# A cap on the token scatters under way in the second attention stage

## The chip, the cores and the metric

The kernel runs on one core of one Trainium2 chip. The metric is the time of one execution on the device in microseconds (us), as the median of several runs. A profiled execution is a separate run, from which the trace and the profile come.

## The reference, cut to what matters

The program is a deformable convolution with a residual, then an attention block, then a mixture of experts, on an input of 4 images of 256 channels and 64 x 64 positions. After the attention each of the 4 x 4096 = 16,384 tokens (256 values) is normalised, and a router picks two of eight experts for it:

```python
def _moe(tokens, router_w, w1, b1, w2, b2):
    logits = tokens.astype(jnp.float32) @ router_w.astype(jnp.float32).T
    probs = jax.nn.softmax(logits, axis=-1)
    rw, re = jax.lax.top_k(probs, TOP_K)                 # TOP_K = 2
    rw = rw / jnp.maximum(rw.sum(-1, keepdims=True), 1e-12)
    combine = jnp.zeros((N, E), tokens.dtype).at[jnp.arange(N)[:, None], re].set(rw)
    out = tokens
    for e in range(E):                                   # E = 8
        h = jax.nn.gelu(tokens @ w1[e] + b1[e], approximate=False)
        out = out + combine[:, e:e + 1] * (h @ w2[e] + b2[e])
    return out
```

Everything is float32. The kernel does not multiply all tokens by all experts: it sorts each token's row to the two experts that it chose.

## The kernel before, in words

The work runs in four stages, one after the other with small overlaps.

1. The deformable convolution. POOL (GpSimd) gathers four corners of each sample by indirect DMAs (L626), VectorE weighs them (L651), PE transposes and multiplies (L665, L690).
2. The first attention stage (from L819): statistics, queries and keys, and the 4 x 4 attention weights `att` between the images for each head.
3. The second attention stage (L1071 to L1509), which the change touches. `block(j)` (L1291) is called for j = 0 to 7; a block is 512 positions of all four images, 2,048 tokens or 16 tiles of 128. For each block PE makes the values and the gates (`value`, `gate`, both through `project`, L796), ScalarE and VectorE mix the images (`spread` L1091, `mixed` L1098), VectorE gates (`gated`, L1118), PE multiplies by the output matrix (`output`, L1129), VectorE adds the residual (`added`, L1146), and ScalarE takes squares (`squares`, L1165). The routing of block j - 1 is woven into block j: POOL raises the variances to the power -1/2 (`rstd`, L1178, twice a block), VectorE makes the shift (L1185) and picks two experts (`pick`, L1206 to L1224), ScalarE normalises the rows into the tile `u` (`normed`, L1193), PE counts tokens by expert (`count`, L1238), and VectorE turns that into row numbers (`placed`, L1252 to L1264).
4. The experts (from L1516): 142 tiles of 256 sorted rows are fetched (`fetch`, L1531), multiplied (`hidden` L1577, `result` L1595), and their results are scattered back (L1606).

A scatter (`scatter`, L1273) is an indirect DMA that POOL issues: it writes the 128 rows of one tile, 260 words each, to the rows `xs_rows` in DRAM whose numbers stand in `slots`. There are 16 tiles and 2 choices for each of 8 blocks, so 256 scatters; `placed` puts 32 of them in the list `waiting`, and `scatter(n)`, called at fixed places in `block`, takes up to n of them from it. The scatters of the last block are issued one for each expert tile in stage 4 (L1737).

What sets the order: in the second attention stage the order of VectorE, ScalarE, PE and SyncE is that of the text (`manual_schedule`, L836); POOL's is left to the scheduler. `in_turn` (L181) adds edges of order, without a wait, between the scatters and the `rstd` instructions: `scatter` puts each scatter behind the last `rstd` issued, and `rstd` goes behind all the scatters issued since the one before. In stage 4 POOL's order is that of the text too.

All scatters write to one of two DRAM tensors. They write disjoint rows, so each is declared to be free of dependencies towards the others in a group named "scatter" (L1281, L1282).

The DMAs that POOL issues take turns on eight semaphores, and each waits, before it is issued, for the earlier one that counted on its own semaphore.

Of the kernel before, what the change touches and what calls it, by code (L numbers as in the profile page):

```python
# [67 lines left out]
RELOADED = -(-(NE * WROW + SPARE * HALF) // (B * STATE))  # L68
FETCH = 3
XTS, YS = 5, 4  # L70
NG = B * NT


# [5 lines left out]
def conv_attn_moe_kernel(  # L79
# [101 lines left out]
    def in_turn(ins, others):  # L181

        for other in others if not fixed else ():
            tc.add_manual_dep(
                ins.ins, other.ins.name,
                mybir.DependencyInfo(mybir.DependencyClass.NoSync, mybir.DependencyReason.DATA),
                reason="order of issue",
            )
# [36 lines left out]
    with ExitStack() as actx:  # L225
# [482 lines left out]
        with tc.manual_schedule(engines=order):  # L708
# [7 lines left out]
            for n in range(total + 2):  # L716
# [22 lines left out]
                if n % 2 == 0 and n + NGB < total:  # L739
# [6 lines left out]
                        reason="the next gather's buffer",  # L746
# [266 lines left out]

    gates = route_pool.tile([P, NBLK, 2, NG], F32, name="gates")
    rank_i = route_pool.tile([P, NE], I32, name="rank_i")
# [16 lines left out]

    same_expert = route_pool.tile([P, NE, NG], F32, name="same_expert")
    G.memset(same_expert, 1.0)
# [14 lines left out]
    def over_experts(ap):  # L1049
        return ap.unsqueeze(2).to_broadcast([P, NG, NE])  # L1050

    def over_tiles(ap):
        return ap.unsqueeze(1).to_broadcast([P, NG, NE])

    def first_max(pool, lg, name, which):

        m = pool.tile([P, NG], F32, name=f"m{which}_{name}", tag=f"top_m{which}")
        V.tensor_reduce(m, lg, AX.X, ALU.max)
        oh = pool.tile([P, NG, NE], F32, name=f"oh{which}_{name}", tag=f"top_oh{which}", bufs=1)
        V.tensor_tensor(oh, lg, over_experts(m), ALU.is_equal)  # L1060
# [10 lines left out]
    with ExitStack() as bctx:  # L1071
# [172 lines left out]

        waiting = []
        scattered = []

        def placed(j):
            pp, oh1, oh2 = picked.pop(j)
            base = bases[j - 1] if j % HB else base0  # L1250
            pos = bs.tile([P, NG, NE], F32, name=f"pos{j}", tag="lg", bufs=1)
            V.tensor_tensor(  # L1252
                pos, pp[:, : NE * NG].rearrange("p (e n) -> p n e", n=NG), over_tiles(base),
                ALU.add,
            )
            after = bs.tile([P, NE], F32, name=f"base{j}", tag="base")
            V.tensor_tensor(after, pp[:, NE * NG : NE * NG + NE], base, ALU.add)
            bases[j] = after
            slots = bs.tile([P, 2, NG], I32, name=f"slots{j}", tag="slots")
            for k, oh in enumerate((oh1, oh2)):  # L1260
                V.tensor_tensor(oh, oh, pos, ALU.mult)
                row = bs.tile([P, NG], F32, name=f"row{j}_{k}", tag="row")
                V.tensor_reduce(row, oh, AX.X, ALU.add)
                V.tensor_copy(slots[:, k], row)  # L1264
            waiting.extend(
                (us[j, n // NT], slots, n, k, xs_rows[j // HB])
                for n in range(NG) for k in range(2)
            )

        def scatter(most):  # L1270
            for _ in range(min(most, len(waiting))):
                u, slots, n, k, rows_ = waiting.pop(0)
                s = G.indirect_dma_start(  # L1273
                    out=rows_,
                    out_offset=bass.IndirectOffsetOnAxis(ap=slots[:, k, n : n + 1], axis=0),
                    in_=u[:, n % NT, :], in_offset=None,
                )
                in_turn(s, issued[-1:])
                scattered.append(s)

                tc.declare_no_dep(s.ins, group="scatter", reason="disjoint rows")  # L1281
                tc.add_to_no_dep_group("scatter", s.ins)  # L1282
# [8 lines left out]
        def block(j):  # L1291
# [25 lines left out]
            mixed(j, 1, 1, [2, 3])  # L1317
            spread(j, 0, [1, 0])
            scatter(3)
            scatter(10)  # L1320
            mixed(j, 1, 1, [0])
            gate(j, 1, 1)
# [18 lines left out]
            value(j, 2, 0)  # L1341
            mixed(j, 3, 0, [0])
            scatter(13)
            mixed(j, 3, 0, [2])
            mixed(j, 2, 0, [1])
# [447 lines left out]
```

## Time and profile before

| what | us |
|---|---|
| three timed runs | 3581.35, 3588.42, 3590.16 |
| their median | 3588.42 |
| the profiled execution | 3621.63 |
| its span, from the first instruction to the last | 3619.9 |
| convolution, until the last gather (L626) | to about 2114 |
| first attention stage | about 2114 to 2392 |
| second attention stage, until its last `rstd` pair begins | about 2392 to 2917 |
| experts and output | from about 2917 on |

How to read the profile: PE is the matrix engine and PEld its weight load, DVE is VectorE, ACT is ScalarE, POOL is GpSimd, SP is SyncE; a "q" behind an engine's name (POOLq) is its sequencer, which waits and issues. A group line gives source line, engine, operation, what it writes and reads, the count, then its busy time and the mean of one in ns, and then the time that the engine stood idle just before such instructions and who ended that idle time. "issue" there means that the profile shows nothing that was waited for; "remote" or "an unknown queue" means that a semaphore was waited for whose update the profile cannot assign to an instruction. The row of an indirect DMA on POOL is the time of its issue by POOL; the packets of the data stand in the view of the DMA engines.

### The profile page before, as it was taken

The numbers are of one execution on the slowest core, as the hardware profiler recorded it, in microseconds if no ns is written. First come the engines' busy times: TensorE is split into PE (matmuls) and PEld (weight loads), VectorE is DVE, ScalarE is ACT, GpSimd is POOL, SyncE is SP. The second block draws the span as 40 slices with busy tenths as digits, with TensorE's granted clock in tenths as the row PEclk, the third lists the DMA queues.
The fourth block names the chain that finished last, engine by engine and source line by source line (L and its number), as shares of the span: only waits on it lengthen the run. The fifth ranks groups of instructions, "written<-read, shape, count | busy, mean of one in ns | idle before, by whom it ended". The sixth has DMA issues, their size and how long they took to land.

```text
span 3619.9 us, 49496 instructions
## 1 busy us (share of the span) xinstructions
PE 3041.8 (84%) x13658; PEld 2230.4 (62%) x13658; DVE 2480.5 (69%) x6303; ACT 1832.4 (51%) x4281; POOL 1961.6 (54%) x1818
## 2 busy tenths in 40 slices
PE   5899997899987899977777889997676588899996
PEld 4667665667665676656566655543343367788884
DVE  5867686777776777866666758875445555455887
ACT  2556554456554565544444457744344254455663
POOL 2555565666576665677666643305445536655441
PEclk8999998999998999989888989998788789999996
DMA  9889889899989899988787878723234334444888
GB/s 301 306 304 336 316 326 351 278 353 366 348 313 350 307 346 341 352 297 310 280 312 285 320 205 141 139 74 121 99 105 154 111 97 132 154 138 153 289 280 285
DMA packets 349897, 911.66 MB, mean 252 GB/s; under 512 B 43540, under 2 KB 123035, under 8 KB 347576
## 3 DMA queue, kind: packets, MB, share of 16 engines
q0 software_dynamic: 208704, 689.10, 55.1%
q1 hardware_dynamic: 140920, 219.39, 19.0%
q8 instruction: 113, 1.85, 0.2%
q14 instruction: 160, 1.31, 0.1%
HBM read 741.87 MB, written 170.12 MB: 252 GB/s over the span
## 4 chain that ended last, share of the span: by engine, by line
PE 48%; issue 14%; POOL 11%; DMA 9%; DVE 8%; another core or an unknown queue 6%; ACT 3%; SPq 0%; POOLq 0%; DVEq 0%; ACTq 0%
PE acc L690 13%; POOL g L626 10%; DMA g<-table,idx 6%; PE ph L1577 6%; PE py L1595 5%; PE tps L665 3%; PE po L433 3%; PE po L1129 3%; DVE s L651 3%; PE p_wq_sb L796 3%; PE p_wk_sb L796 3%; PE pg L796 2%; PE pv L796 1%; DVE mix L1098 1%
## 5 line engine op out<-in xcount | busy, mean ns | idle before, releaser
L651 DVE SCALAR_TENSOR_TENSOR s<-g,wts,s 128x256 f32<-128x256 f32 x3456 | 1433.5, 479 | 542.3 <-ACT s L643 374.3
L626 POOL DMA_INDIRECT g<-table,idx x1152 | 1310.4, 1137 | 765.7 <-DVE s L651 465.2
L690 PE MATMUL acc<-wconv_sb,sT 128*128 128x265 f32 x4608 | 1338.9, 415 | 274.3 <-ACT sT L671 165.7
L690 PEld LDWEIGHTS acc<-wconv_sb,sT 128*128 128x128 f32 x4608 | 832.4, 201 | 423.5 <-ACT sT L671 196.2
L671 ACT COPY sT<-tps 128x256 f32<-128x256 f32 x1152 | 425.4, 369 | 781.0 <-PE tps L665 489.9
L643 ACT ACTIVATE s<-g,wts 128x256 f32<-128x256 f32 x1152 | 588.9, 511 | 210.2 <-DMA g<-table,idx 180.9
L665 PE MATMUL tps<-ident,s 128*128 128x128 f32 x2304 | 461.7, 283 | 39.8 <-DVE s L651 37.8
L665 PEld LDWEIGHTS tps<-ident,s 128*128 128x128 f32 x2304 | 327.7, 148 | 270.1 <-issue 162.4
L1606 POOL DMA_INDIRECT ys_rows<-y,to x284 | 282.9, 996 | 299.9 <-DVE y L1603 225.2
L1577 PE MATMUL ph<-xT,w 128*128 128x256 f32 x1136 | 282.8, 392 | 35.6 <-DVE second L1563 18.3
L1273 POOL DMA_INDIRECT xs_rows<-u,slots x256 | 250.0, 976 | 94.6 <-issue 88.8
L1595 PE MATMUL py<-w,hT 128*128 128x256 f32 x1136 | 270.7, 381 | 0.0
L1581 ACT ACTIVATE hT<-ph,w 128x256 f32<-128x256 f32 x284 | 132.7, 474 | 237.2 <-PE ph L1577 170.0
L1577 PEld LDWEIGHTS ph<-xT,w 128*128 128x128 f32 x1136 | 210.3, 196 | 66.6 <-ACT hT L1581 18.4
L1600 DVE TENSOR_TENSOR y<-py,w 128x512 f32<-128x512 f32 x142 | 98.2, 691 | 206.8 <-ACT w L1539 70.7
L1595 PEld LDWEIGHTS py<-w,hT 128*128 128x128 f32 x1136 | 218.3, 192 | 30.5
L1098 DVE SCALAR_TENSOR_TENSOR mix<-pv,att,mix 128x512 f32<-128x512 f32 x192 | 131.0, 742 | 142.6 <-remote 106.3
L1103 ACT ACTIVATE gate<-pg,bg_c 128x512 f32<-128x512 f32 x64 | 43.8, 688 | 277.1 <-DVE mix L1118 190.1
L919 DVE SCALAR_TENSOR_TENSOR junk<-q,k 128x512 f32<-128x512 f32 x256 | 162.1, 687 | 24.6 <-ACT k L900 24.4
L433 PE MATMUL po<-xs,woff_sb 128*96 128x512 f32 x288 | 152.4, 612 | 0.0
L796 PE MATMUL pg<-early_state,wg_sb 128*128 128x512 f32 x160 | 87.1, 680 | 76.9 <-DVE mix L1098 61.8
L1178 POOL TENSOR_TENSOR rstd<-l3var,nhalf 128x8 f32<-128x8 f32 x16 | 26.5, 1656 | 215.1 <-DVE l3var L1176 207.2
(264 smaller groups left out, 3432.1 us busy)
## 6 DMA issues: line engine op xcount, KB each, us to landing
xt<-xs_rows SPq DMA_DIRECT2D x142, 260.0 KB
table<-zt SPq DMA_DIRECT2D x96, 256.0 KB
yk<-ys_rows SPq DMA_DIRECT2D x80, 256.0 KB
g<-table,idx POOLq DMA_INDIRECT x1152
t<-o SPq DMA_DIRECT2D x32, 530.0 KB
t<-bo_sb POOLq DMA_DIRECT2D x32, 530.0 KB
dt<-t SPq DMA_DIRECT2D x64, 265.0 KB
xraw<-in_x SPq DMA_DIRECT2D x16, 1024.0 KB
```

The source lines that it names most:

```text
L433: T.matmul(t["po"], woff_sb[:, ch, ki].rearrange("p kj o -> p (kj o)"), t["xs"][:, ch, ki : ki + RB], start=(n == 0), stop=(n == NCH * 3 - 1),
L626: g = G.indirect_dma_start(out=gs[n % NGB], out_offset=None, in_=tables[b], in_offset=bass.IndirectOffsetOnAxis(ap=params[b][0][:, r, k : ...
L643: first = S.activation(ss[n], gs[n % NGB][:, :C], AF.Copy, scale=params[b][1][:, 0, r, k : k + 1])
L651: last_corner[n] = V.scalar_tensor_tensor(ss[n], gs[n % NGB][:, c * C : (c + 1) * C], params[b][1][:, c, r, k : k + 1], ss[n], ALU.mult, A ...
L665: T.transpose(tps[n][:, ch * P : (ch + 1) * P], s[:, ch * P : (ch + 1) * P], ident)
L671: S.copy(sTs[n], tps.pop(n))
L690: T.matmul(accs[n // K2][:, :CR], sT[:, ch * P : (ch + 1) * P], wconv_sb[:, ch, k, :], start=False, stop=(k == K2 - 1 and ch == NCH - 1),)
L796: T.matmul(ps, w[:, ci, ch * P : (ch + 1) * P], src[:, ci, :], start=(ci == 0), stop=(ci == NCH - 1),)
L1273: s = G.indirect_dma_start(out=rows_, out_offset=bass.IndirectOffsetOnAxis(ap=slots[:, k, n : n + 1], axis=0), in_=u[:, n % NT, :], in_off ...
L1577: T.matmul(ph, w1_sb[:, ch, f * P : (f + 1) * P], xT[:, ch, :], start=(ch == 0), stop=(ch == NCH - 1),)
L1595: T.matmul(py[:, i, :], hT[:, f, i * P : (i + 1) * P], w2_sb[:, f, :], start=(f == 0), stop=(f == NCH - 1),)
L1606: s = G.indirect_dma_start(out=ys_rows[g], out_offset=bass.IndirectOffsetOnAxis(ap=to[:, i : i + 1], axis=0), in_=y[:, i, :], in_offset=No ...
```

## The change

A constant and a list are added, and in `scatter` a dependency with a wait is requested from each scatter on the scatter four in front of it. The declaration of the group "scatter", in the two lines below, stays as it was.

```diff
+AT_A_TIME = 4
...
         waiting = []
         scattered = []
+        every = []
...
                 in_turn(s, issued[-1:])
                 scattered.append(s)
 
+                every.append(s)
+                if len(every) > AT_A_TIME:
+                    tc.add_manual_dep(
+                        s.ins, every[-1 - AT_A_TIME].ins.name,
+                        mybir.DependencyInfo(
+                            mybir.DependencyClass.Sync, mybir.DependencyReason.DATA
+                        ),
+                        reason="room for its descriptors",
+                    )
+
                 tc.declare_no_dep(s.ins, group="scatter", reason="disjoint rows")
                 tc.add_to_no_dep_group("scatter", s.ins)
```

## The prediction

> **What bounds the kernel now.** I read the page's chain first, then the stage that holds the scatters, then the scatters' own lines, then the DMA engines beside them.
>
> The last-ending chain of the whole program, by engine:
>
> ```profile
> span 3619.9 us, 49496 instructions
> ...
> PE 48%; issue 14%; POOL 11%; DMA 9%; DVE 8%; another core or an unknown queue 6%; ACT 3%; SPq 0%; POOLq 0%; DVEq 0%; ACTq 0%
> ...
> L1273 POOL DMA_INDIRECT xs_rows<-u,slots x256 | 250.0, 976 | 94.6 <-issue 88.8
> ...
> L1098 DVE SCALAR_TENSOR_TENSOR mix<-pv,att,mix 128x512 f32<-128x512 f32 x192 | 131.0, 742 | 142.6 <-remote 106.3
> ```
>
> The token scatters (L1273) are 250.0 us of POOL and do not stand in the chain's line list at all. What does stand there is 6% from "an unknown queue"; a large part is VectorE's: 106.3 us of idle time ahead of the mixes of L1098 whose releaser the profile does not name. So the scatters matter to the end only if they are what holds VectorE up, or if they become slow enough to delay what POOL does behind them.
>
> The table of stretches, one row for each interval between POOL's `rstd` instructions (one block of the stage each). Columns: length, then busy time of each engine:
>
> ```profile
> 2437.18:2491.37 54.19, 44.83 (x136) 26.22 (x135) 33.77 (x77) 26.83 (x76) 21.77 (x22) 0.91 0.36 126
> ...
> 2564.22:2637.00 72.78, 47.03 (x137) 26.29 (x135) 34.08 (x77) 27.18 (x77) 34.47 (x35) 0.79 0.31 103
> ```
>
> Both blocks do the same arithmetic (VectorE 33.8 and 34.1 us), yet the one with 32 scatters beside it takes 18.6 us longer than the one with 19. That is the time somebody could hope for. POOL itself is busy 34.5 of 72.8 us and is not the bound.
>
> **What the change does to the program: nothing.** The edit adds to each scatter, from the fifth on (256 - 4 = 252 of them), a dependency on the scatter four in front. But a few lines further on, each scatter is put into the group "scatter", whose members are declared to have no dependency on each other (disjoint rows); both ends of the new edge are members. In the two built programs, laid beside each other, POOL's 1,823 listed instructions stand in the same order and each waits for the same semaphores at the same values, and so it is on the other engines; only source line numbers differ. A scatter waits, in both, for the one of eight DMA semaphores that it will itself count on, which is the landing of the eighth scatter in front. No wait for the fourth is there. Nothing is removed, added or moved: on PE, VectorE, ScalarE, POOL and the DMA queues the cost is 0 us, and it needs no cover.
>
> **What it would cost if the wait were there** (the bounds, should the dependency come into the program after all). The line view of L1273, columns min/median/max in ns, first and last start:
>
> ```profile
> L1273 POOL DMA_INDIRECT xs_rows<-u,slots x256: 956/963/1613, 2454.8 to 3158.6; - x128
> L1273 POOLq EVENT_SEMAPHORE  x68: 17/17/13756, 2440.2 to 3073.4; - x68
> ```
>
> and two rows of POOL's timeline in one block (start, length, idle before):
>
> ```profile
> 2607.24 0.96 POOL L1273 DMA_INDIRECT xs_rows<-u,slots  x1 [0.30 <-issue]
> 2608.50 0.96 POOL L1273 DMA_INDIRECT xs_rows<-u,slots  x1 [0.30 <-issue]
> ```
>
> A scatter starts every 0.96 + 0.30 = 1.26 us. A wait for the fourth in front can hold it only if that one lands later than 4 x 1.26 = 5.0 us after its own start; the wait for the eighth holds only beyond 10.1 us, and the rows never show more than the usual 0.30 us, so landing takes less than 10.1 us. How much less, the DMA engines tell. Their view over 2601 to 2613 us, in 40 slices of 0.3 us, the last scatter of the block being the one of 2608.50:
>
> ```profile
> DMA  5600380009100830066004700290009200000000
> ...
> DMA packets 384, 1.07 MB, mean 89 GB/s; under 512 B 128, under 2 KB 128, under 8 KB 384
> ...
> q0 software_dynamic: 384, 1.07, 24.9%
> ```
>
> Each burst is one scatter: 1.07 MB in 8 bursts is 133 KB each, 128 rows of 260 words. The bursts are short and the slices between them are empty: the queue is drained before the next scatter reaches it. The last burst ends in the 32nd slice, so by 2601 + 32 x 0.3 = 2610.6 us, 2.1 us after the start of the last scatter. So about 2.1 / 1.26 = 1.7 scatters are under way at a time, and a cap of four does not act. A real wait would then cost one semaphore instruction for each scatter: 252 x 17 ns = 4.3 us of POOL, 0.5 us a block, beside the 27 us that POOL idles ahead of the next `rstd` (its timeline shows 27.39 us there). Upper bound of that form: each costs a whole gap of 0.30 us, 9.6 us a block, still inside those 27 us. On the path that is 0 to 4.3 us; I take 0, since the wait is not in the program.
>
> Two rules of the Trainium skill bear on this reading. The row gives 963 ns for a scatter; the page "Perfetto Trace Analysis", section "DMA Instruction — SWDGE (GPSIMD)", says that such a row ends when the last descriptor is written, not when the data has landed. By the row alone 0.8 scatters would be under way, by the bursts above 1.7; the sum is 0 by either.
> The scatters run beside VectorE's long mixes and still take 956 to 1,613 ns. The page "SBUF — State Buffer", section "SBUF: two separate sides", warns that GpSimd cannot write descriptors while VectorE runs a two-port operation, and its section "A bandwidth-pool intuition that's wrong" gives 3,100 ns in place of 620 for such a DMA; an estimate by that page is 2.5 us more for a scatter so caught, a landing of some 4.6 us, which would make the cap of four nearly act, against 0 by the rows, where no scatter of the 256 is stretched so.
>
> **The rivals.**
> *Faster.* The wait is real after all, more than four scatters are under way somewhere, and spacing them out ends VectorE's unexplained stops. For it: the stops (7.31, 7.10 and 11.21 us in the chain of the block 2564 to 2637) stand only where scatters run, and the blocks without a full set of them are 18.6 us shorter. Against it: the program holds no such wait, and the bursts show 1.7 under way. Price: all 106.3 us of the L1098 row, 3588.4 - 0.991 x 106.3 = 3483 us.
> *Slower.* The wait is real and takes the place of the issue gap: behind a waiting scatter stand, on POOL, the other scatters of the block, then the two `rstd` of the next statistics, for which VectorE's `shift` and the whole choice of experts wait. It decides from a landing of 5.0 us on. At the far bound, 10.1 us, a scatter would start every 10.1 / 4 = 2.53 us: 32 x 2.53 + 3.3 (two `rstd`) + 1.3 (gap between them) = 85.6 us a block. From the `rstd` at 2491.4 to that at 2917.2 lie six blocks, 425.8 us; they would take 513.6: +87.8 us, 3588.4 + 0.991 x 87.8 = 3675 us. Against it: the same bursts.
>
> **How the numbers follow.** The profiled execution took 3621.63 us (span 3619.9 and 1.7 around it), 0.9% above the median 3588.42 of the three timed runs; so a sum made on the profile is scaled by 0.991. The sum is 3621.63 + 0, scaled 3588 us. Two times of one program can still differ: the three runs lie from 3581.35 to 3590.16, 0.25% apart, and about 0.3% (10.8 us) is what a measurement of this kernel can tell from no change. Chances: the same program 0.96, of which 0.92 within 0.3%, 0.02 above and 0.02 below by chance of the timing; the faster rival 0.02, the slower 0.02. That gives faster 0.04, same 0.92, slower 0.04. A range of 0.3% to each side, 3577 to 3599, leaves 0.08 out and takes in the 4.3 us of a wait that is there and never holds.
>
> **What would show it.** In the changed kernel the scatter stands two lines lower. Right: its line again has 256 scatters of about 963 ns with 0.30 us between them, 68 semaphore instructions, blocks of 72.8 us, some 106 us of unnamed idle time ahead of the mixes. Wrong, the wait is there: some 252 semaphore instructions more at that line. Wrong and binding: gaps above 0.30 us between scatters, released by the DMA of the scatters, and either a longer block or stops of VectorE that are gone.

## The result and the profile after

| kernel | median, us | runs | lowest to highest |
|---|---|---|---|
| before | 3596.59 | 20 | 3573.39 to 3617.11 |
| after | 3595.84 | 20 | 3569.02 to 3626.7 |

The ratio is 0.9996, with a 95% interval from 0.9977 to 1.0015: no change that this measurement can tell. The page of the kernel after, with the lines that answer to those shown of before:

```profile
span 3591.9 us, 49496 instructions
...
PE 48%; issue 13%; POOL 12%; DMA 8%; DVE 8%; another core or an unknown queue 6%; ACT 3%; SPq 0%; POOLq 0%; ACTq 0%; DVEq 0%
...
L1275 POOL DMA_INDIRECT xs_rows<-u,slots x256 | 250.2, 977 | 94.7 <-issue 87.7
...
L1099 DVE SCALAR_TENSOR_TENSOR mix<-pv,att,mix 128x512 f32<-128x512 f32 x192 | 131.0, 742 | 142.9 <-remote 130.7
```

The instruction count is the same, 49,496. The scatters cost the same 250 us of POOL, and VectorE still loses 130.7 us ahead of its mixes to a releaser that the profile does not name (106.3 before). The two spans differ by 28 us, but 24 of these have already arisen when the changed stage begins: its first `rstd` starts at 2412.85 us here and at 2437.18 before. That is the convolution, which the change does not touch. The table of stretches between `rstd` instructions, for the same two blocks as before (length, then the busy time of PE, PEld, VectorE, ScalarE, POOL; granted clock, DMA share, GB/s):

```profile
2412.85:2467.09 54.24, 44.79 (x136) 26.19 (x135) 33.84 (x77) 26.81 (x76) 22.13 (x22) 0.91 0.36 126
2540.25:2612.65 72.40, 46.80 (x136) 26.09 (x135) 34.08 (x77) 27.04 (x77) 34.15 (x35) 0.79 0.31 104
```

The blocks were 54.19 and 72.78 us long, and are 54.24 and 72.40. The seven of the stage add up to 478.8 us, before to 480.0. Last the scatter's own line, with its sequencer's semaphore instructions:

```profile
L1275 POOL DMA_INDIRECT xs_rows<-u,slots x256: 954/960/1607, 2430.4 to 3133.5; - x128
L1275 POOLq EVENT_SEMAPHORE  x68: 17/17/13760, 2415.8 to 3043.0; - x68
```

There are 68 semaphore instructions, as before. This count alone would not settle it: e1 below, which does have the wait, shows 70 of them and 49,497 instructions. What settles it is the order and the waits. Every engine runs the same instructions in the same order in the two traces, and of the 256 scatters 180 stand behind a wait on the semaphore of the eighth scatter in front in both; 13 stand behind one on that of the fourth before, 12 after. In e1 it is 35 for the eighth and 149 for the fourth.

### The profile page after: what moved, and what is told of

It is laid out like the page before. It is cut to its first block, busy times and chain, and to the rows that moved or that the text cites. A ratio compares the mean times of both kernels' runs of the same rounds, so it can differ in the third digit from the quotient of the medians.

```text
span 3591.9 us, 49496 instructions
## 1 busy us (share of the span) xinstructions
PE 3036.8 (85%) x13658; PEld 2230.5 (62%) x13658; DVE 2479.6 (69%) x6303; ACT 1832.3 (51%) x4281; POOL 1966.8 (55%) x1818
## 4 chain that ended last, share of the span: by engine, by line
PE 48%; issue 13%; POOL 12%; DMA 8%; DVE 8%; another core or an unknown queue 6%; ACT 3%; SPq 0%; POOLq 0%; ACTq 0%; DVEq 0%
PE acc L691 12%; POOL g L627 11%; DMA g<-table,idx 6%; PE ph L1589 6%; PE py L1607 5%; PE po L434 4%; DVE s L652 4%; PE tps L666 3%; PE p_wq_sb L797 3%; PE po L1130 3%; PE p_wk_sb L797 3%; PE pg L797 3%; PE pv L797 2%; PE tpx L1568 1%
## 5 line engine op out<-in xcount | busy, mean ns | idle before, releaser
L1099 DVE SCALAR_TENSOR_TENSOR mix<-pv,att,mix 128x512 f32<-128x512 f32 x192 | 131.0, 742 | 142.9 <-remote 130.7
```

## The experiments

The prediction rested on two legs: the dependency does not come into the program, and it would cost nothing if it did. The runs made the wait real, at four caps, and then asked why a smaller cap changes the time. This table holds all twelve; the text behind it takes them in groups. "Stage" is the sum of the seven blocks of the profiled execution (480.0 before). "Stops" is the idle time ahead of VectorE's mixes alone with no named releaser, the 106.3 us of before; that of other engines and instructions is not in it. "Start to start" is the median distance of two scatters in the stage (1.27 us before). The runs were made on four chips, on which the kernel before took 3599.81, 3543.25, 3537.1 and 3606.61 us, so only ratios are set side by side. The times of some 3,500 to 3,531 us in the expectations of e5, e6 and e7 start from the chip of e1 to e4 (3599.81) and can't be held against those runs, which were made beside 3543.25.

| run | what | us, of before | ratio, 95% interval | stage | stops | start to start |
|---|---|---|---|---|---|---|
| e1 | wait for the 4th in front, real | 3590.87, 3599.81 | 0.9975 [0.9944, 1.0006] | 472.3 | 107.2 | 1.27 |
| e5 | for the 3rd | 3510.49, 3543.25 | 0.9891 [0.9844, 0.9938] | 425.0 | 32.2 | 1.27 |
| e2 | for the 2nd (one time) | 3530.86, 3599.81 | none | 407.3 | 0 | 1.48 |
| e6 | for the 2nd, timed | 3470.97, 3543.25 | 0.979 [0.9758, 0.9821] | 417.3 | 0 | 1.46 |
| e3 | for the one in front | 3789.43, 3599.81 | 1.053 [1.0487, 1.0572] | 691.4 | 0 | 2.88 |
| e4 | no cap, each behind a VectorE instruction | 3527.16, 3599.81 | 0.9794 [0.9756, 0.9831] | 411.7 | 0 | 1.27 |
| e7 | e4 with the cap of 2 | 3535.5, 3543.25 | 0.9978 [0.9954, 1.0002] | 482.4 | 0 | 1.84 |
| e8 | no cap, a pause of 0.57 us on POOL | 3505.0, 3543.25 | 0.9886 [0.9857, 0.9914] | 431.4 | 0 | 1.83 |
| e9 | no cap, one fill of 0.11 us | 3530.75, 3537.1 | 0.9978 [0.9956, 0.9999] | 455.8 | 87.5 | 1.27 |
| e10 | the fill between the gathers instead | 3562.77, 3537.1 | 1.0057 [1.0032, 1.0083] | 461.9 | 102.9 | 1.27 |
| e11 | no cap, two fills | 3494.62, 3606.61 | 0.9708 [0.9672, 0.9744] | 371.1 | 0 | 1.38 |
| e12 | no cap, four fills | 3537.66, 3606.61 | 0.9837 [0.98, 0.9874] | 430.5 | 0 | 1.70 |

The stage of one profiled execution is a weak measure: in e10, where the stage is that of before, it is 461.9 us, 18 less. Differences of that size are not read below.

### The wait made real: caps of four, three, two and one (e1, e5, e2, e6, e3)

To keep the edge, the scatters take turns in eight groups in place of the one, and each declares itself free of all groups but that of the scatter for which it is to wait:

```diff
+AT_A_TIME = 4          # 3 in e5, 2 in e2 and e6, 1 in e3
+TURNS = 8
...
-                tc.declare_no_dep(s.ins, group="scatter", reason="disjoint rows")
-                tc.add_to_no_dep_group("scatter", s.ins)
+                i = len(every)
+                every.append(s)
+                late = (i - AT_A_TIME) % TURNS if i >= AT_A_TIME else None
+                if late is not None:
+                    tc.add_manual_dep(s.ins, every[i - AT_A_TIME].ins.name, ...)
+                for group in ("fill", *(f"scatter {t}" for t in range(TURNS) if t != late)):
+                    tc.declare_no_dep(s.ins, group=group, reason="disjoint rows")
+                tc.add_to_no_dep_group(f"scatter {i % TURNS}", s.ins)
```

The writes of `no_row`, which were in the old group too, go into "fill" and are declared free of all the others. In the traces the wait for the n-th scatter in front takes, for most scatters, the place of the wait for the eighth. The number of instructions hardly changes: 49,489 to 49,540 in the five, beside 49,496.

> The wait for the fourth scatter in front is made real: the scatters are put into eight groups in turn, and each declares itself free of dependencies towards all groups but that of the scatter four in front. In the built program each scatter now waits on the semaphore of the scatter four in front, in place of the one eight in front. Theory (a scatter lands some 2.1 us after its start, so the cap of four never holds): same time, within 0.3% of the kernel before; scatters 0.30 us apart as before, blocks of some 72 us, some 106 to 131 us of unnamed idle time ahead of the mixes. Rival 'faster' (a cap of four ends VectorE's stops): some 100 us less. Rival 'slower' (landing takes more than 5.0 us): gaps above 0.30 us between scatters, up to 88 us more.

Measured: 0.9975 [0.9944, 1.0006]. From the list of waits of e1 (total us, times, longest us):

```profile
DVE mix L1100 <- remote: 107.2, 13, 16.2
...
POOL xs_rows L1276 <- DMA xs_rows<-u,slots: 9.2, 27, 1.2
```

The wait is there now: 27 scatters have the landing of another as the last thing waited for (17 times and 5.2 us before). But all of these waits but one, of 1.22 us, end within the usual gap of 0.30 us, the scatters still start every 1.27 us, and VectorE's stops stay. So a real cap of four changes nothing that can be measured. That leg held.

> As the run before, with a wait for the second scatter in front, so two under way at most. Theory (landing 2.1 us, period 1.26 us): 2 x 1.26 = 2.5 us is still more than 2.1, so gaps stay at 0.30 us for most scatters and the time within 0.5% of before. If landing really takes between 2.5 and 5.0 us: a start every landing/2, so 1.3 to 2.5 us, visible as gaps above 0.30 us.

The expectation was wrong: the cap of two was faster. One time decides little, so it was timed again.

> The kernel with the wait for the second scatter in front once more, now timed in five rounds, because its single look gave 3531 us where the expectation was no change. If that was no accident: 0.978 to 0.985 of before, idle time ahead of the mixes some 14 us, blocks of some 59 us.

Measured: 0.979 [0.9758, 0.9821]. POOL's timeline of e6 (start, length, idle time before and its releaser) and, from its page, the mixes:

```profile
2561.08 0.96 POOL L1276 DMA_INDIRECT xs_rows<-u,slots  x1 [0.42 <-DMA xs_rows<-u,slots]
2562.45 0.96 POOL L1276 DMA_INDIRECT xs_rows<-u,slots  x1 [0.41 <-DMA xs_rows<-u,slots]
2563.80 0.96 POOL L1276 DMA_INDIRECT xs_rows<-u,slots  x1 [0.39 <-DMA xs_rows<-u,slots]
2565.62 0.96 POOL L1276 DMA_INDIRECT xs_rows<-u,slots  x1 [0.86 <-DMA xs_rows<-u,slots]
```

```profile
L1276 POOL DMA_INDIRECT xs_rows<-u,slots x256 | 254.2, 993 | 196.1 <-DMA xs_rows<-u,slots 126.6
...
L1100 DVE SCALAR_TENSOR_TENSOR mix<-pv,att,mix 128x512 f32<-128x512 f32 x192 | 129.8, 741 | 13.2 <-ACT mix L1093 9.5
```

POOL now loses 126.6 us to landings, and the program is 2.1% faster. The mixes' idle time falls from 142.6 to 13.2 us, and none of it is unnamed. The gaps of 0.39 to 0.86 us in place of 0.30 are small, so the distance of two scatters grows by only 0.1 to 0.6 us.

> A real wait for the third scatter in front. The run with a wait for the first one showed a start-to-start time of 2.7 us in a quiet stretch (0.96 us of issue, some 1.76 us of waiting), up to 4 us in a busy one; so a scatter lands 2.4 to 3.7 us after its start. Three periods of 1.27 us are 3.8 us: the wait holds hardly ever. Theory (what counts is that the wait lengthens the period): time within 0.5% of before, unnamed idle time ahead of the mixes 80 us or more. Rival (a bound on the number under way counts by itself): near the 3531 us of the wait for the second.

The cap of three stands between: 0.9891 [0.9844, 0.9938], a little faster than the 0.5% that the theory allowed, and short of the cap of two. The mixes' stops are 32.2 us, but other instructions stop more than before: ScalarE's gates 82.1 us (16.4 before) and the residual's sums 51.0 us (4.2). The scatters still come in trains, up to 15 in a row that start less than 1.30 us apart (30 before, at most 2 at the cap of two).

> As before, with a wait for the landing of the scatter just in front, so one under way. Theory: the wait now holds on every scatter, and the start-to-start time measures the landing: 2.1 to 2.6 us. 32 x 2.3 + 4.6 us for the rstd pair makes a block 78 us instead of 72.8 if VectorE's stops have nothing to do with how densely scatters follow each other: some 30 us slower over six blocks. Rival (the dense train of scatters is what stops VectorE): the unnamed idle time ahead of the mixes falls well below 100 us, and the block is then bound by POOL alone at some 78 us, or less if the scatters of the last blocks slide into the expert stage.

Measured: 1.053 [1.0487, 1.0572], 189.6 us more, several times the loss that was expected. With one scatter under way, the distance of two is the time from a scatter's start until its landing is seen and the next one starts. POOL's timeline of e3:

```profile
2561.05 0.96 POOL L1276 DMA_INDIRECT xs_rows<-u,slots  x1 [2.24 <-ACT u L1160]
2563.73 0.96 POOL L1276 DMA_INDIRECT xs_rows<-u,slots  x1 [1.72 <-DMA xs_rows<-u,slots]
2567.13 0.96 POOL L1276 DMA_INDIRECT xs_rows<-u,slots  x1 [2.44 <-DMA xs_rows<-u,slots]
2569.87 0.96 POOL L1276 DMA_INDIRECT xs_rows<-u,slots  x1 [1.78 <-DMA xs_rows<-u,slots]
```

The distances are 2.68, 3.40 and 2.74 us. With the median of 2.88, a block is 32 x 2.88 + 4.6 (the two `rstd` and their gap) = 96.8 us of POOL alone; the blocks measured 97.6 to 105.2 us, apart from the first. So the chain of scatters on POOL sets the length of the block, with VectorE's stops gone (0 us).

What follows from the five: the stops are gone once no long train of scatters is left, at the caps of two and one, and a spacing beyond what POOL has time for costs more than the stops. What stays open is whether it is the number under way or the pace that matters, or where among VectorE's work the scatters stand.

### Where the scatters stand, without a cap (e4, e7)

```diff
-                V.scalar_tensor_tensor(o, pvs[j, t_, ch], a, o, ALU.mult, ALU.add)
+                scatter(1, V.scalar_tensor_tensor(o, pvs[j, t_, ch], a, o, ALU.mult, ALU.add))
...
-        def scatter(most):
+        def scatter(most, behind=None):
...
+                if behind:
+                    tc.add_manual_dep(s.ins, behind.ins.name, ...)
...
-            scatter(3)
-            scatter(10)
...
-            scatter(13)
...
-            scatter(5)
...
-            scatter(1)
```

The other eight of a block go behind the residual's last sums (L1147) in the same manner. e7 has the cap of two as well.

> No cap; instead the 32 scatters of a block are spread over it, each behind one VectorE instruction (24 mixes, 8 residual additions), so that they come one by one and not in a train of 32. All scatters and all bytes stay. If the dense train is what stops VectorE (7, 7 and 11 us in a block of 72.8): the stops shrink, the block falls towards 54 us, up to 18 x 6 = 108 us less. If the number of scatters is what counts, or the stops have another cause: block and time as before.

Measured: 0.9794 [0.9756, 0.9831], as fast as the cap of two. The stops of the mixes are gone, but trains of scatters at 1.27 us remain where several VectorE instructions end close together (up to 13 in a row), and there are unnamed stops at other places. The list of waits of e4:

```profile
ACT gate L1103 <- remote: 96.7, 7, 19.2
...
PEld po L1129 <- remote: 62.9, 11, 7.8
...
DVE early_state L1146 <- remote: 45.7, 7, 9.5
```

Before, ScalarE's gates had 16.4 us of these, and the residual's sums 4.2. The stops have moved with the trains. That they belong to the trains and not to the mixes is the likeliest reading.

> Both remedies together: the scatters in step with VectorE's instructions and a wait for the second in front. In step alone, stretches of 1.27 us between scatters are left, and ScalarE, VectorE and PE still have unnamed idle time (97, 78 and 63 us in the stage). Theory (a dense train is the cause): these shrink and the time falls below both, 3500 to 3525 us. If each remedy already takes all that there is: 3525 to 3531 us. If POOL becomes the bound by the longer periods: above 3531 us.

Both together gain nothing: 0.9978 [0.9954, 1.0002]. The stops are away, but the scatters start every 1.84 us. ScalarE waits 105.3 us for scatters to free the tiles `u` that it is to write, and VectorE's `shift` waits 76.6 us for `rstd` (12.2 before).

### The pace without any wait (e8, e9, e11, e12)

The cap does two things: it bounds the number under way, and it slows the pace. A pause on POOL slows the pace and waits for no landing:

```diff
+PAUSE = 1
...
+    pause = plan_pool.tile([P, PAUSE], F32, name="pause")
...
+                if not fixed:
+                    paused.append(G.tensor_tensor(pause, ones[:, :PAUSE], nhalf[:, :PAUSE], ALU.pow))
+                    in_turn(paused[-1], scattered[-1:])
...
+                in_turn(s, paused[-1:])
```

e9 has `G.memset(pause, 0.0)` in place of the power, e11 two and e12 four of these in a row. The group "scatter" is that of before, and the wait is the old one for the eighth in front.

> No cap and no step: a small instruction of POOL's own (a power of one value a partition, an estimate of some 0.6 us from the 726 ns of two values) stands between any two scatters of the second attention stage. So the period is longer, while nothing waits for a landing. Theory (the pace decides, not the wait): period 1.6 to 1.9 us, unnamed idle time ahead of the mixes below 40 us, 0.975 to 0.99 of before. Rival (the wait for a landing is what helps): as before, within 0.5%.

Measured: 0.9886 [0.9857, 0.9914], the stops 0 us, with no wait for a landing at all (none stands in the waits of the scatter's line). So a slower pace removes the stops without the wait. Two rows of e8's POOL, and what takes the stops' place (waits, total, times, longest):

```profile
2570.51 1.04 POOL L1280 DMA_INDIRECT xs_rows<-u,slots  x1 [0.19 <-issue]
2571.57 0.57 POOL L1278 TENSOR_TENSOR pause<-ones,nhalf 128x1 f32<-128x1 f32 x1
```

```profile
ACT u L1161 <- DMA xs_rows<-u,slots: 112.6, 12, 12.5
...
DVE l3var L1179 <- ACT u L1168: 89.1, 7, 18.5
```

A scatter starts every 1.83 us, so 32 of them take 58.6 us of a block of 63, and two `rstd` take 3.3 more. POOL itself is the new bound: in three blocks from 2435 us on the chain that ends last stays on POOL. So ScalarE's `u` tiles come free late, and VectorE's variances wait for ScalarE.

> As the run with a power between any two scatters, but with a memset of one value a partition in its place, which should be shorter (the memsets of two values took 0.10 to 0.12 us here). With the power the period was 1.83 us, the unnamed idle time was gone, but ScalarE then waited 112.6 us for scatters to free the tiles u. Theory (any period clearly above 1.27 us ends the stops, and a shorter one frees u earlier): period 1.35 to 1.5 us, no unnamed idle time, blocks of 56 to 60 us instead of 62.9, 0.975 to 0.983 of before. Rival (some 1.7 us are needed): unnamed idle time comes back, above 0.99 of before.

Measured: 0.9978 [0.9956, 0.9999], next to no change. One fill fits into the gap that is there anyway. POOL's timeline of e9:

```profile
2499.69 0.96 POOL L1280 DMA_INDIRECT xs_rows<-u,slots  x1 [0.19 <-issue]
2500.65 0.11 POOL L1278 MEMSET pause<- 128x1 f32 x1
2500.95 0.96 POOL L1280 DMA_INDIRECT xs_rows<-u,slots  x1 [0.19 <-issue]
```

The distance is 1.26 us, as without the fill, and the stops are 87.5 us; ScalarE's gates stop for another 128.5 us (16.4 before). The expectation of 0.975 to 0.983 was wrong because the period did not grow. This makes it the control for the next two: an instruction between the scatters does nothing as long as the pace stays.

> Two fills of 128x1 between scatters, no cap. One fill (0.11 us) disappeared in the gap of 0.30 us, so that scatters still started every 1.27 us. If each further one adds some 0.12 to 0.2 us (an estimate from the fill's own 0.11 us), they start every 1.4 to 1.5 us. Theory that the pace of the scatters holds VectorE up: VectorE's stops without a named releaser ahead of the mixes fall from 87 to 106 us to below 50, ratio 0.985 to 0.995. Rival, that the gain of the earlier pause came from something else than the pace (what it computes, the shared port): stops as before and 0.998.

Measured: 0.9708 [0.9672, 0.9744], more than was expected (0.985 to 0.995), and the best of all kernels here. POOL's timeline, the mixes on the page, and the block's row in the table of stretches:

```profile
2517.83 0.96 POOL L1282 DMA_INDIRECT xs_rows<-u,slots  x1
2518.79 0.27 POOL L1279 MEMSET pause<- 128x1 f32 x2
2519.21 0.96 POOL L1282 DMA_INDIRECT xs_rows<-u,slots  x1
```

```profile
L1101 DVE SCALAR_TENSOR_TENSOR mix<-pv,att,mix 128x512 f32<-128x512 f32 x192 | 129.8, 741 | 16.7 <-ACT mix L1094 9.5
```

```profile
2521.78:2574.91 53.13, 46.20 (x135) 25.89 (x136) 33.74 (x78) 29.70 (x85) 40.99 (x99) 0.94 0.38 122
```

The distance is 1.38 us, a mere 0.12 us more, and no engine has an unnamed stop in the whole stage. The block lasts 53.1 us, not 72.8, with the same work of PE and VectorE, and the stage 371.1 us, not 480.0: 109 us, beside 112 us in the medians. The clock granted to PE is higher here (0.94, before 0.79), but PE's busy time in the block differs by only 0.8 us (46.20 and 47.03), so the clock does not make up the 19.7 us. ScalarE's wait for `u` is 58.7 us, about half of e8's 112.6.

> Four fills of 128x1 between scatters, no cap: a scatter every 1.65 to 1.85 us (an estimate from the fill's 0.11 us). By the pace: the stops ahead of the mixes below 20 us, as with the pause of 0.6 us, and ratio 0.98 to 0.99; the rest of the gain is lost on ScalarE, which waits longer for the scatters to free its buffers. By the rival: stops of 87 to 106 us, and 0.998 or more.

Measured: 0.9837 [0.98, 0.9874], with a distance of 1.70 us, the stops 0, and ScalarE's wait for `u` back at 112.6 us. That is as expected.

e9, e11 and e12 differ in the number of fills alone. The stops end somewhere between 1.27 and 1.38 us of distance, and wholly; from 1.38 to 1.70 us some 1.3% of the time is lost again.

### The same between the gathers (e10)

```diff
+        pause = asm.tile([P, 1], F32, name="pause", bufs=1)
...
+            if n >= NGB:
+                G.memset(pause, 0.0)
```

The gathers of the convolution come at the same pace as the scatters, and ScalarE has 202.9 us of unnamed stops there.

> The same small memset, not between the scatters but between the gathers of the convolution stage; the scatters are as before. There, ScalarE's copies show 181 us of idle time with an unnamed releaser. If dense gathers hold back PE's signals as dense scatters do, and if that is on the path: 20 to 150 us less, and that idle time falls. If the gathers' own rate bounds that stage (POOL's gathers are 11% of the chain of the end and the transfers 6%): 0 to 100 us more, since 1152 gathers come each some 0.1 to 0.2 us later.

Measured: 1.0057 [1.0032, 1.0083], slower by 0.6%. The fill vanishes in the gap here too (gathers still start 1.25 us apart where they are densest), so the run does not try the pace. ScalarE's unnamed stops were 152.3 us; but in e9, whose convolution is that of before, they were 144.3. Whether a real pause would help the gathers stays open; two fills were not tried there.

## Why the prediction was right

- *The edge is dropped.* Right: the same instructions in the same order, the same waits for the eighth scatter in front, the same blocks, ratio 0.9996. That 149 scatters of e1 do wait for the fourth, once the two ends are in different groups, shows that the group was what removed the edge. The sign that was named for being wrong, some 252 semaphore instructions more, would not have come: e1 has the wait and 70 of them. (The profile counts 1,818 instructions of POOL in both kernels; where the 1,823 of the prediction come from is not on record.)
- *A real wait for the fourth would cost 0 to 4.3 us.* Right in its result: e1 gave 0.9975 with 1 in its interval. The price named was for a separate semaphore instruction; there is next to none (two more in e1), since the new wait takes the place of the old one.
- *Landing some 2.1 us after the start, 1.7 scatters under way.* Too low. e3 gives 2.7 to 3.4 us until the landing is seen and the next scatter starts, that is 2.1 to 2.7 under way at 1.27 us. The step that failed is reading the landing from the end of the data's burst: the signal that POOL waits for is later. The threshold of 5.0 us for a cap of four was nevertheless hardly ever reached: one wait of e1 went beyond the usual gap. The rows before do show three gaps above 0.30 us (12.92, 4.65 and 0.87 us), unlike what the prediction read, but none of them ends with a landing. The figure of 2.1 us would have misled for smaller caps: by 2.1 us a cap of two (2.5 us) does not act, and it does, with 126.6 us of waits.
- *The faster rival.* That spacing ends the stops is real, and its price was about right: 3483 against 3588 us is 0.971, and e11 measured 0.9708. That they agree so closely is luck: the price counted only the mixes' stops, while e11 also ended those of other engines and paid 58.7 us of ScalarE's waiting for `u`. And it took a pace of 1.38 us; no bound on the number under way was needed. The prediction was right to hold that a cap of four does not reach it. Its argument against the rival, that only 1.7 scatters are under way, did not bear on it: spacing helps although the queue is drained. Of the three stops that it quoted, the chain gives that of 7.10 us as "issue", so it is not in the 106.3 us.
- *The slower rival.* Its form was right: a period of landing by cap, and POOL as the bound from there. e3 shows it at a cap of one with a block of 96.8 us worked out and 97.6 to 105.2 measured. At a cap of four a landing of more than 5.0 us would be needed, and only one wait of e1, of 1.22 us, held a scatter longer than the usual gap.
- *The Trainium skill's rule on blocked descriptor writes ("SBUF — State Buffer", "SBUF: two separate sides").* The scatters beside VectorE's mixes took 954 to 1,607 ns in the kernel after; an issue of 3,100 ns is not to be seen. The estimate of 4.6 us for a landing that was worked out from it lies above the 2.7 to 3.4 us of e3, and the cap of four did not act. The rule itself is not tested here, since no run shows that the mixes are two-port operations.

## What to carry to other kernels

When an edit adds a dependency, look whether both ends are in a group that is declared free of dependencies among its members: then nothing is added, and the program, not the diff, says so: look at what each instruction waits for, since a count of instructions can miss a wait that takes the place of another. When an engine has stops whose releaser the profile does not name, look what else runs in just those blocks, and lengthen its pace by a tenth of a microsecond before adding any wait: here two fills of 128x1 gave more than every cap. A control that leaves the pace as it is (e9) tells the pace from the mere presence of the added instruction.

## What the runs showed of the hardware

A train of scatters at 1.27 us on POOL goes with stops of the other engines; at 1.38 us and above, in e2, e6, e8, e11 and e12, the stage has none. VectorE's timeline of the kernel after, in one such train, shows them:

```profile
2567.10 2.73 DVE L1099 SCALAR_TENSOR_TENSOR mix<-pv,att,mix 128x512 f32<-128x512 f32 x4 [7.92 <-remote]
2576.89 2.07 DVE L1099 SCALAR_TENSOR_TENSOR mix<-pv,att,mix 128x512 f32<-128x512 f32 x3 [7.06 <-remote]
2590.19 2.07 DVE L1099 SCALAR_TENSOR_TENSOR mix<-pv,att,mix 128x512 f32<-128x512 f32 x3 [11.24 <-remote]
```

The chain of waits has the same three stretches as "another core or an unknown queue" (7.89, 7.04 and 11.21 us), on the path that sets the block's end. They are 26 us of a block that becomes 19 us shorter when they are gone. What the mixes wait for is PE's values. The kernel before shows it in two of its views, PE's timeline and that of all engines:

```profile
2579.64 6.60 PE L796 MATMUL pv<-early_state,wv_sb 128*128 128x512 f32 x15
...
2591.18 1.41 DVE L1098 SCALAR_TENSOR_TENSOR mix<-pv,att,mix 128x512 f32<-128x512 f32 x2 [7.34 <-remote]
```

By 2586.24 us the matmuls of four values have ended, those of the first at 2581.09, and yet PE's semaphore, on which these mixes wait, is counted up only at 2591.15. The trace's records of semaphore updates show the same at all the unnamed stops of the mixes, 11 before and 15 after: each ends 0.02 to 0.03 us after an update of PE's semaphore, and each of these updates comes 2.0 to 23.3 us after the last recorded matmul that counts on it. In the whole stage PE's recorded updates come up to 24.0 us late before, but at most 1.9 us in e11, and the median is 0.01 us in both; those of VectorE and ScalarE come at most 0.9 us after their instructions in both. So what a train at 1.27 us goes with is a late signal of PE. Two reservations stay: the ends of matmuls are modelled, and not every update is recorded (149 of PE's for 179 instructions that count in the stage before). Why 0.12 us of distance decides, whether a shared path for semaphore updates fills up or something else does, stays open.
